# Spectral ffn image by image: groups of 16 bins and bursts of four steps in a ring of half PSUM banks

## The chip, the cores and the metric

The kernel runs on one core of a Trainium2 chip. The metric is the device time of the execution in microseconds; lower is better. Three runs of the kernel before gave 2106.07, 2108.23 and 2112.26 us (median 2108.23). All data are fp32.

## What is computed

x has shape (2, 128, 64, 64). Three blocks follow one another; the change touches only the last one.

```python
x = x + conv_ref(_gn(x), ...)                 # neighbourhood attention and an mlp
t = _to_tokens(x)                             # (2, 4096, 128)
t = t + attn_ref(_ln_t(t))                    # full attention over 4096 tokens
t = t + ffn_ref(_ln_t(t), ...)                # spectral filter ("stu")

# ffn_ref, for one branch:
Vf = rfft(phi, n=8192, axis=0)                # 16 filters in time
Uf_p = rfft(u, n=8192); Uf_m = rfft(u * sgn, n=8192)
U_plus  = irfft(Vf * Uf_p)[:sl]
U_minus = irfft(Vf * Uf_m)[:sl] * sgn
out = einsum('btkd,k,kde->bte', U_plus, s, Mpp) + einsum('btkd,k,kde->bte', U_minus, s, Mpm)
out = out + three short lags u[t-i] @ Mu[i]
```

Four such branches (over the whole, half, quarter and eighth of the sequence) are weighted by a hard softmax choice.

## The kernel before

Layer 0 and the attention of layer 1 come first, up to about 1296 us of the trace. While attention runs on image 1, the spectra of the tokens are stored to a DRAM tile `us` (line 1045 and 1050) and those of the filters to a DRAM tile `gs`; the matrices `mpl` and `mmi` (16 matrices of 128 by 128 each, sum and difference of the two sets) and the inverse transform `inv` are made in SBUF.

The last stage is the ffn in the frequency domain. There are `K2` = 80 indices q, each with four bins (j = 0 to 3). Both images are worked on together. One group takes `KG` = 2 indices (kl), so there are 40 groups.

- **Loads** (`blocks`, line 1335, and `inputs`, line 1405). For each kl SyncE issues four DMAs for the filter block `ct` (40 or 32 KB) and one for `ut`, the spectra of both images (256 KB, pieces of 2 KB). Four kl are loaded ahead, in five buffers.
- **Burst** (line 1430). A Toeplitz product of filter block and spectrum, for one kl and one image: for par 0 and 1, four products with 32 contraction rows each (row slices of the array, j = 0 to 3), 256 columns, into four PSUM banks. par 0 and par 1 fill the two interleaved parts of the same four banks. Then four copies of 128 by 512 (line 1438) bring the banks to `y`, j even on VectorE, j odd on ScalarE. A group has four bursts (two kl times two images); they compute the `y` of the following group.
- **Projection** (line 1450). 32 products with 128 contraction rows, 256 columns, accumulate `acc` over l (mpl, mmi) and the 16 filters. A burst for the next group stands ahead of every eight projections.
- **Mixed bins** (lines 1458 to 1477). ScalarE copies `acc` to `af`; POOL (VectorE in the last group) forms eight sums and differences and puts them into `ob` (the first 64 indices) or `ob_last` (the other 16).
- **Back transform** (`back_into`, lines 1484 to 1500). When 64 indices are done, each of the 16 places (image, par, f) gets four transposes into one bank, one copy to `t`, then four products with `inv` and two adds into the residual `xa`. These steps are slipped in behind projections k = 5 and 13, in groups 32 to 39.
- **Tail** (lines 1548 to 1592). Behind the last group: 16 transposes of `ob_last`, then four turns (half h, image b) of residual products, 32 products with `inv`, eight copies or adds into `o` and a store of 1 MB.

TensorE's order in the loop is the order of the program text (`manual_schedule`); the other engines' instructions are ordered by the framework. PSUM has eight banks of 512 fp32 columns: here `ps_c` is a ring of six banks for bursts, transposes and back products, and `ps_p` two buffers for `acc`. An fp32 product shows in the trace as two TensorE instructions.

Of the kernel before, what the change touches and what calls it, by code (L numbers as in the profile page):

```python
# [96 lines left out]
KG = 8 // FB  # L97
GB = 4 * KG
# [5 lines left out]
def kernel(  # L104
# [1290 lines left out]
    with ExitStack() as cv:  # L1395
        cp = cv.enter_context(tc.tile_pool(name="conv", bufs=5))
        ps_c = cv.enter_context(tc.tile_pool(name="ps_c", bufs=6, space=PSUM))
        ps_p = cv.enter_context(tc.tile_pool(name="ps_p", bufs=2, space=PSUM))
        def lag_bank():
            return ps_c.tile([P, 512], F32, tag="pc", name="py")  # L1400

        def inputs(q):

            ut = cp.tile([P, NB, 2, P], F32, tag="ut", name="ut")
            nc.sync.dma_start(
                out=ut.rearrange("p b s d -> p (b s d)"),
                in_=us[2 * q : 2 * q + 2].rearrange("g n i r f b s d -> (g n i r f) (b s d)"),
            )
            return ut

        TK = FB * KF
        GROUPS = K2 // KG
        NX = 8 // FB
        UNITS = [(kl, images) for kl in range(KG) for images in (((0,), (1,)) if FB == 4 else ((0, 1),))]
        taken = []

        def burst(y, i):

            kl, images = UNITS[i]
            if images[0] == 0:  # L1420
                taken[:] = ahead.pop(0)
            ct, ut = taken
            pcs = [ps_c.tile([P, 2, 2 * NX, TK], F32, tag="pc", name="pc") for _ in range(4)]
            for i_, b in enumerate(images):
                for par in range(2):
                    cv_ = ct[:, :, 0 : 2 * (FB + 1 + par) * KF].rearrange("p o (l c) -> p o l c", l=2)[:, :, :, 0:TK]
                    at = slice(2 * i_ + par, 2 * i_ + par + (NX - 1 if par else NX + 1) + 1, NX - 1 if par else NX + 1)
                    for j in range(4):
                        rows_ = slice(32 * j, 32 * j + 32)
                        nc.tensor.matmul(  # L1430
                            pcs[j][:, :, at, :], lhsT=ut[rows_, b, par, :], rhs=cv_[rows_], start=True, stop=True
                        )
            for j in range(4):
                if FB == 4:
                    to = y[:, :, :, 4 * kl + j, images[0] * 2 * FB : (images[0] + 1) * 2 * FB]
                else:
                    to = y[:, :, :, 4 * kl + j, :]
                (nc.scalar.copy if j % 2 else nc.vector.tensor_copy)(  # L1438
                    to, pcs[j].rearrange("p o (l x) (t k) -> p (o l) k (x t)", l=2, k=KF)
                )  # L1440
            if to_load and images[-1] == 1:
                q_ = to_load.pop(0)
                ahead.append((blocks(q_), inputs(q_)))

        def new_y():
            return cp.tile([P, 4, KF, GB, 4 * FB], F32, tag="y", name="y", bufs=2)

        def project(g, y, acc, l, k):

            nc.tensor.matmul(  # L1450
                acc, lhsT=(mmi if l else mpl)[:, k, :],
                rhs=y[:, l::2, k], start=(l == 0 and k == 0), stop=(l == 1 and k == KF - 1),
            )

        def mixed_bins(g, acc):
# [3 lines left out]
            eng = nc.gpsimd if g + 1 < GROUPS else nc.vector  # L1459
            av = af.rearrange("p (m s x) -> p s m x", s=2, x=4 * FB)  # L1460
            sd = cp.tile([P, 2, 128], F32, tag="sd", name="sd", bufs=2)
            for s, op in enumerate((ALU.add, ALU.subtract)):
                to = sd[:, s, :].rearrange("p (o x k) -> p o k x", o=2, x=4 * FB)
                a_, b_ = (av[:, i].rearrange("p (o k) x -> p o k x", o=2) for i in range(2))
                eng.tensor_tensor(to, a_, b_, op)  # L1465
            sv, dv = (sd[:, s].rearrange("p (o x k e) -> p e o x k", o=2, k=KG, e=2) for s in range(2))
            c, k0 = divmod(g * KG, BC)
            if c < K2 // BC:
                to = [ob[:, c, a].rearrange("p x k o -> p o x k")[:, :, :, k0 : k0 + KG] for a in range(4)]
            else:  # L1470
                to = [ob_last[:, :, a].rearrange("p x k o -> p o x k")[:, :, :, k0 : k0 + KG] for a in range(4)]
            eng.tensor_tensor(to[0], sv[:, 0], sv[:, 1], ALU.add)
            eng.tensor_tensor(to[1], sv[:, 0], sv[:, 1], ALU.subtract)
            eng.tensor_tensor(to[2][:, 0], dv[:, 0, 0], dv[:, 1, 1], ALU.subtract)
            eng.tensor_tensor(to[2][:, 1], dv[:, 0, 1], dv[:, 1, 0], ALU.add)
            eng.tensor_tensor(to[3][:, 0], dv[:, 0, 0], dv[:, 1, 1], ALU.add)
            eng.tensor_tensor(to[3][:, 1], dv[:, 0, 1], dv[:, 1, 0], ALU.subtract)

        def back_into(chunk, b, par, f):

            pt = ps_c.tile([P, 4, P], F32, tag="pc", name="pt")
            for a in range(4):
                src = ob[:, chunk, a, (b * 2 + par) * FB + FB - 1 - f]
                nc.tensor.transpose(pt[:, a, :], src.rearrange("p k o -> p (k o)"), ident)
            t = cp.tile([P, 4, P], F32, tag="t", name="t", bufs=4)
            nc.scalar.copy(t, pt)
            yield True
            na = 512 // CQ
            for a0 in range(0, 4, na):
                py = ps_c.tile([P, na, CQ], F32, tag="pc", name="py")  # L1490
                for a in range(na):
                    nc.tensor.matmul(
                        py[:, a, :], lhsT=t[:, a0 + a, :], rhs=inv[:, 4 * chunk + a0 + a, :], start=True, stop=True
                    )
                xv = xa[b][:, par * TH : (par + 1) * TH].rearrange(
                    "p (h x e f c l) -> p x f e l h c", x=NFP, e=2, f=2, c=64, l=2
                )[:, f // 2, f % 2]
                for a in range(0, na, 2):
                    xs = xv[:, (a0 + a) // 2]
                    nc.vector.tensor_tensor(xs, py[:, a : a + 2, :].rearrange("p l (h c) -> p l h c", c=64), xs, ALU.add)  # L1500
                yield None if a0 + na == 4 else True

        places = [(b, par, f) for b in range(NB) for par in range(2) for f in range(FB)]
        to_load = list(range(K2))
        ahead = [(ct, inputs(to_load.pop(0))) for ct in first_blocks]
        rest = []
        with tc.manual_schedule(engines={mybir.EngineType.PE}):
            y = new_y()
            for i in range(4):
                if i % 2 == 0:  # L1510
                    next(lags, None)
                burst(y, i)
# [6 lines left out]
            ob = obp.tile([P, K2 // BC, 4, 4 * FB, BC, 2], F32, name="ob")  # L1519
            ob_last = obp.tile([P, 4 * FB, 4, LAST, 2], F32, name="ob_last")  # L1520
            for g in range(GROUPS):
                following = new_y() if g + 1 < GROUPS else None
                acc = ps_p.tile([P, 256], F32, tag="acc", name="acc")
                for l in range(2):
                    for k in range(KF):
                        if following is not None and k % 8 == 0:
                            burst(following, 2 * l + k // 8)
                        project(g, y, acc, l, k)
# [3 lines left out]
                mixed_bins(g, acc)  # L1532
                y = following
                if (g + 1) * KG % BC == 0:
                    rest += [back_into(g * KG // BC, *p) for p in places]
# [5 lines left out]

        turned_ = {}
        for b in range(NB):
            for par in range(2):
                pt = ps_c.tile([P, FB, P], F32, tag="pc", name="pt")
                for f in range(FB):
                    src = ob_last[:, (b * 2 + par) * FB + FB - 1 - f]
                    nc.tensor.transpose(pt[:, f, :], src.rearrange("p a k o -> p (a k o)"), ident)
                turned_[b, par] = cp.tile([P, 4, P], F32, tag="t", name="t", bufs=4)
                nc.scalar.copy(turned_[b, par][:, 0:FB], pt)  # L1550
        HQ = CQ // 2
        for h in range(2):
            for b in range(NB):
                o = cp.tile([P, HQ, 2, 2, FB, 2], F32, tag="o", name="o", bufs=2)
                pys = [ps_c.tile([P, 2, FB, HQ], F32, tag="pc", name="py") for _ in range(4)]
                xv = [
                    xa[b][:, par * TH + h * (TH // 2) : par * TH + (h + 1) * (TH // 2)].rearrange(
                        "p (h x e f c l) -> p e l x f h c", x=NFP, e=2, f=2, c=64, l=2
                    )
                    for par in range(2)  # L1560
                ]

                def residual(par, a):
                    v = xv[par][:, a // 2, a % 2]
                    return v[:, :, :, 0] if FB == 4 else v[:, 0]

                def alike(v):
                    return v.rearrange("p (x f) c -> p x f c", f=2) if FB == 4 else v.rearrange("p f (h c) -> p f h c", c=64)

                for a in (0, 2):  # L1570
                    for par in range(2):
                        nc.tensor.matmul(
# [115 lines left out]
```

## Time and profile before

| what | value |
|---|---|
| median of three runs | 2108.23 us |
| the profiled execution's own time | 2109.33 us |
| its span in the trace | 2107.4 us |
| TensorE granted clock, mean | 0.992 |
| span before the first burst of the ffn | 1295.85 us |
| first to last projection | 1307.3 to 2078.9 us |
| behind the last projection | 28.5 us |

Times are microseconds from the span's start. PE is TensorE's products, PEld its weight loads, DVE is VectorE, ACT ScalarE, POOL GpSimd, SPq the DMA-issuing queue of SyncE. A timeline row has start, duration, engine, line, operation, names as output<-inputs, shapes, a count, and in brackets the engine's idle time before it and what ended it. A row of waits has the waiting engine, its tile and line, what it waited for, the total, the number of times and the longest. A row of stretches has, behind its length, each engine's busy time with its instructions in the order PE, PEld, DVE, ACT, POOL, then the granted clock, the DMA engines' busy share and GB/s.

### The profile page before, as it was taken

To read this page: it belongs to the slowest core of one execution; us is meant where nothing else is said; L and a number is where in the kernel's file an instruction comes from. 1 tells how busy PE (TensorE), PEld (TensorE's weight loads), DVE (VectorE), ACT (ScalarE), POOL (GpSimd) and SP (SyncE) were. 2 spreads that over 40 slices of the span, in tenths; PEclk is the share of its full clock that TensorE was granted. 3 is DMA by queue.
4 is the path that set the end of the run, shared out by engine and by line. 5 is a ranking of instruction groups with operands and counts; after the bars stand their busy time and mean duration, and the time that the engine had idled before them with its cause. 6 is when DMAs were issued, how large, how long until landed. Compare 5 with 4: busy or idle time off the path is not lost.

```text
span 2107.4 us, 36450 instructions
## 1 busy us (share of the span) xinstructions
PE 2042.4 (97%) x13704; PEld 1336.8 (63%) x13704; DVE 962.1 (46%) x3368; ACT 727.1 (35%) x1942; POOL 397.0 (19%) x703
## 2 busy tenths in 40 slices
PE   6899998999999999999999999999999999999998
PEld 4677775554555554554455555777777777777877
DVE  5799986444543455346534455222222222222332
ACT  3788985222322233122222322222222222222222
POOL 3366976214000000000000000110111111110100
PEclk8999999999999999999999999999999999999999
DMA  4222223012000011004200013111111111111102
GB/s 148 62 61 61 62 60 54 6 42 83 22 4 25 26 41 57 4 27 124 70 8 18 26 51 99 40 48 41 46 43 45 48 40 48 41 46 40 40 9 81
DMA packets 181839, 99.96 MB, mean 47 GB/s; under 512 B 70927, under 2 KB 169375, under 8 KB 181152
## 3 DMA queue, kind: packets, MB, share of 16 engines
q1 hardware_dynamic: 180738, 94.13, 16.1%
q8 instruction: 109, 1.79, 0.3%
q0 software_dynamic: 576, 2.10, 0.3%
q10 hardware_dynamic: 350, 1.41, 0.3%
q14 instruction: 66, 0.54, 0.1%
HBM read 62.98 MB, written 34.63 MB: 46 GB/s over the span
## 4 chain that ended last, share of the span: by engine, by line
PE 82%; DVE 6%; DMA 4%; POOL 4%; ACT 1%; issue 1%; SPq 1%; ACTq 0%; DVEq 0%; POOLq 0%
PE acc L1450 28%; PE own L958 10%; PE bank L920 9%; PE pc L1430 8%; PE other L985 8%; PE bank L944 4%; PE bank L345 2%; PE bank L203 1%; PE bank L555 1%; PE bank L1060 1%; DMA st<-in_m_plus_dram 1%; DMA st<-in_m_minus_dram 1%; PE bank L1103 1%; ACT p L542 1%; PE bank L519 1%
## 5 line engine op out<-in xcount | busy, mean ns | idle before, releaser
L1438 DVE COPY y<-pc 128x512 f32<-128x512 f32 x320 | 206.2, 686 | 514.9 <-PE pc L1430 395.4
L928 ACT ACTIVATE e<-bank 128x512 f32<-128x512 f32 (+3 forms) x288 | 161.7, 561 | 518.9 <-PE bank L920 396.0
L1438 ACT COPY y<-pc 128x512 f32<-128x512 f32 x320 | 171.8, 589 | 445.5 <-PE pc L1430 432.2
L1450 PE MATMUL acc<-y,mpl 128*128 128x256 f32 x1280 | 299.9, 385 | 0.0
L1450 PE MATMUL acc<-y,mmi 128*128 128x256 f32 x1280 | 299.9, 385 | 0.0
L920 PE MATMUL bank<-cm 128*128 128x512 f32 (+3 forms) x576 | 277.7, 565 | 1.4 <-DVE y L666 1.4
L1450 PEld LDWEIGHTS acc<-y,mpl 128*128 128x128 f32 x1280 | 235.5, 190 | 54.1 <-issue 25.9
L1450 PEld LDWEIGHTS acc<-y,mmi 128*128 128x128 f32 x1280 | 235.5, 190 | 54.1 <-issue 25.9
L958 PE MATMUL own<-et,tok 128*128 128x512 f32 x448 | 230.3, 600 | 7.6 <-DVE part L947 7.3
L985 PE MATMUL other<-e,tok 128*128 128x512 f32 x448 | 229.3, 594 | 4.6 <-DVE xa L997 4.6
L947 DVE CUSTOM_DVE_ANT_0 et<-bank,one 128x512 f32<-128x512 f32 x224 | 146.1, 687 | 128.8 <-PE bank L944 128.6
L1430 PE MATMUL pc<-ct,ut 32*128 32x256 f32 x2560 | 186.2, 403 | 3.4 <-DMA ut<-us 3.2
L1465 POOL TENSOR_TENSOR sd<-af 128x128 f32<-128x128 f32 x78 | 34.3, 464 | 700.1 <-ACT af L1458 650.7
L958 PEld LDWEIGHTS own<-et,tok 128*128 128x128 f32 x448 | 82.7, 190 | 120.9 <-issue 60.9
L1430 PEld LDWEIGHTS pc<-ct,ut 32*128 32x128 f32 x2560 | 118.2, 185 | 61.4 <-issue 56.1
L175 POOL TENSOR_TENSOR ln_rs<-ln_rs,mhalf 128x4 f32<-128x4 f32 x24 | 24.2, 1010 | 702.8 <-DVE ln_rs L174 702.8
L985 PEld LDWEIGHTS other<-e,tok 128*128 128x128 f32 x448 | 81.7, 190 | 95.2 <-issue 87.3
L944 PEld LDWEIGHTS bank<-ident,e 128*128 128x128 f32 x896 | 103.0, 141 | 46.1 <-issue 39.4
L920 PEld LDWEIGHTS bank<-cm 128*128 128x128 f32 x576 | 94.4, 191 | 54.2 <-issue 39.2
L542 ACT ACTIVATE p<-p,mn 128x196 f32<-128x196 f32 x256 | 114.4, 449 | 14.3 <-DVE mn L532 13.8
L944 PE MATMUL bank<-ident,e 128*128 128x128 f32 x896 | 117.0, 274 | 0.0
L1041 DVE TENSOR_TENSOR ub<-bank,uo 128x256 f32<-128x256 f32 (+1 forms) x192 | 59.5, 372 | 71.1 <-ACT uo L1038 70.2
(246 smaller groups left out, 2419.8 us busy)
## 6 DMA issues: line engine op xcount, KB each, us to landing
ut<-us SPq DMA_DIRECT2D x80, 256.0 KB
us<-ub SPq DMA_DIRECT2D x128, 128.0 KB
vw<-vd SPq DMA_DIRECT2D x256, 49.0 KB
ct<-gs SPq DMA_DIRECT2D x160, 40.0 KB
ct<-gs SPq DMA_DIRECT2D x160, 32.0 KB
vd<-v SPq DMA_DIRECT2D x128, 32.0 KB
st<-in_m_plus_dram SPq DMA_DIRECT2D x16, 256.0 KB
us<-ub SPq DMA_DIRECT2D x128, 32.0 KB
```

Of the source, the lines that this page charges most:

```text
L345: nc.tensor.matmul(pl, lhsT=wg[:, lo : lo + P], rhs=zT, start=True, stop=True)
L542: nc.scalar.activation(p, p, AF.Exp, bias=t[name + "mn"][:, h : h + 1], scale=-1.0, accum_out=t["den"][:, u, h : h + 1],)
L920: nc.tensor.matmul(ps[:, lo:], lhsT=cm[b][:, n * P : (n + 1) * P], rhs=cm[b][:, CHUNKS[c] * 512 + lo : (CHUNKS[c] + 1) * 512], start=True, ...
L928: nc.scalar.activation(e[:, lo:], ps[:, lo:], AF.Exp, bias=0.0, scale=ASCALE, accum_out=part[:, n, c : c + 1])
L944: nc.tensor.transpose(pt[:, k * P : (k + 1) * P], es[k][:, m * P : (m + 1) * P], ident)
L947: nc.vector.tensor_tensor_reduce(et, pt, one, 1.0, 0.0, ALU.mult, ALU.add, part[:, n, a : a + 1])
L958: nc.tensor.matmul(own, lhsT=tok[b][:, n, :], rhs=e, start=first, stop=last)
L985: nc.tensor.matmul(other, lhsT=tok[b][:, 4 * CHUNKS[a] + j, :], rhs=es[j], start=(j == 0), stop=(j == 3))
L1041: nc.vector.tensor_tensor(ub[:, sgn, 0:n], pu[s][:, 0:n], half[:, 0:n], op)
L1430: nc.tensor.matmul(pcs[j][:, :, at, :], lhsT=ut[rows_, b, par, :], rhs=cv_[rows_], start=True, stop=True)
L1438: (nc.scalar.copy if j % 2 else nc.vector.tensor_copy)(to, pcs[j].rearrange("p o (l x) (t k) -> p (o l) k (x t)", l=2, k=KF))
L1450: nc.tensor.matmul(acc, lhsT=(mmi if l else mpl)[:, k, :], rhs=y[:, l::2, k], start=(l == 0 and k == 0), stop=(l == 1 and k == KF - 1),)
```

## The change

- The ffn is done image by image: 20 groups of `KG` = 4 indices (16 bins) for image 0, then 20 for image 1. `ut` holds one image (pieces of 1 KB), so `ct` and `ut` are loaded once for each image and index: 160 times five DMAs instead of 80 times five.
- A burst covers two kl: four steps (kl, par) of four products each, two bursts a group instead of four. The products are the same in number and size (32 of 256 columns a group).
- PSUM is one tile of eight banks with two halves of 256 columns each. Seven banks are a ring of 14 places: place n is bank n mod 7, half (n div 7) mod 2. Each product of a burst has a place of its own, with a copy of 128 by 256: 32 copies a group instead of 16 of twice the size. The eighth bank holds `acc`, in alternating halves.
- `y`, `ob` and `ob_last` are laid out anew; a transpose now reads its source with a stride of four elements.
- The back transform uses two places with two transposes (or products) each where it used a bank. It follows at groups 16 to 19 of each image.
- Image 0's last 16 indices and its output (`finished`) are done in the first groups of image 1, with all four quarters added on VectorE and without residual products. The tail does image 1 alone, with whole banks as before.

```diff
-        ps_c = cv.enter_context(tc.tile_pool(name="ps_c", bufs=6, space=PSUM))
-        ps_p = cv.enter_context(tc.tile_pool(name="ps_p", bufs=2, space=PSUM))
+        ps = cv.enter_context(tc.tile_pool(name="ps_c", bufs=1, space=PSUM)).tile([P, 8, 2, 256], F32, name="ps_c")
+        RING = 7
+        at_slot = [0]
+        def slot():
+            n = at_slot[0]
+            at_slot[0] += 1
+            return ps[:, n % RING, n // RING % 2, :]
...
-        def inputs(q):
-            ut = cp.tile([P, NB, 2, P], F32, tag="ut", name="ut")
+        def inputs(b, q):
+            ut = cp.tile([P, 2, P], F32, tag="ut", name="ut")
...
-        def burst(y, i):
-            kl, images = UNITS[i]
...
+        def burst(y, kls):
+            for kl in kls:
+                ct, ut = ahead.pop(0)
                 for par in range(2):
...
+                    pcs = [slot() for _ in range(4)]
                     for j in range(4):
                         rows_ = slice(32 * j, 32 * j + 32)
                         nc.tensor.matmul(
-                            pcs[j][:, :, at, :], lhsT=ut[rows_, b, par, :], rhs=cv_[rows_], start=True, stop=True
+                            pcs[j].rearrange("p (l o c) -> p o l c", l=2, o=2), lhsT=ut[rows_, par, :], rhs=cv_[rows_],
+                            start=True, stop=True,
                         )
...
+                    for j in range(4):
+                        n = 4 * kl + j
+                        at = slice(2 * n + 1, 2 * n + 33, 31) if par else slice(2 * n, 2 * n + 34, 33)
+                        (nc.scalar.copy if j % 2 else nc.vector.tensor_copy)(
+                            y[:, :, at, :], pcs[j].rearrange("p (l x k) -> p k l x", l=2, k=KF)
+                        )
+                if to_load:
+                    b_, q_ = to_load.pop(0)
+                    ahead.append((blocks(q_), inputs(b_, q_)))
...
+        def finished(b):
+            ts = []
+            for par in range(2):
+                ts.append(turned(b, par))
+                yield True
+            for h in range(2):
+                o = cp.tile([P, HQ, 2, 2, FB, 2], F32, tag="o", name="o", bufs=2)
+                for par in range(2):
+                    pys = [slot().rearrange("p (f q) -> p f q", f=FB) for _ in range(4)]
+                    for f in range(FB):
+                        for a in range(4):
+                            last_products(pys[a], ts[par], h, f, a, True)
+                    for a in range(4):
+                        nc.vector.tensor_tensor(
+                            alike(place_of(o, par, a)), alike(pys[a]), residual(b, par, h, a), ALU.add
+                        )
+                    if par:
+                        send(b, h, o)
+                    yield None if h and par else True
...
+            groups = [(b, g) for b in range(NB) for g in range(GROUPS)]
+            for i, (b, g) in enumerate(groups):
+                final = i + 1 == len(groups)
+                following = None if final else new_y()
+                acc = ps[:, RING, i % 2, :]
                 for l in range(2):
                     for k in range(KF):
-                        if following is not None and k % 8 == 0:
-                            burst(following, 2 * l + k // 8)
-                        project(g, y, acc, l, k)
+                        if following is not None and k == 0:
+                            burst(following, (2 * l, 2 * l + 1))
+                        project(y, acc, l, k)
...
+                if g + 1 == GROUPS and not final:
+                    rest.append(finished(b))
```

## The prediction

> **What bounds the kernel now.** I read the page's busy shares first, then three stretches of the run, then the timeline inside one period of the long stretch.
>
> ```profile
> PE 2042.4 (97%) x13704; PEld 1336.8 (63%) x13704; DVE 962.1 (46%) x3368; ACT 727.1 (35%) x1942; POOL 397.0 (19%) x703
> ...
> 1307.31:1907.60 600.29, 600.29 (x4067) 467.32 (x4065) 163.37 (x254) 147.70 (x285) 70.56 (x248) 1.00 0.17 45
> 1907.60:2078.90 171.30, 171.20 (x1172) 138.69 (x1168) 49.47 (x90) 43.51 (x82) 18.20 (x64) 1.00 0.09 25
> 2078.90:2107.40 28.50, 19.45 (x304) 16.68 (x304) 9.05 (x24) 10.59 (x21) 0.00 (x0) 0.84 0.37 149
> ```
>
> The change lies wholly in the ffn stage, which is those last 800 us: TensorE is busy all through it at full granted clock, VectorE and ScalarE for a quarter, the DMA engines for 0.17. So the stage lasts as long as TensorE's instruction stream, gaps included. The timeline shows one period, a burst of 16 instructions (8 products in two passes) and 16 projection instructions:
>
> ```profile
> 1500.03 1.15 PE L1430 MATMUL pc<-ct,ut 32*128 32x256 f32 x16
> 1501.10 3.72 PE L1450 MATMUL acc<-y,mpl 128*128 128x256 f32 x16
> 1501.19 1.29 DVE L1438 COPY y<-pc 128x512 f32<-128x512 f32 x2 [3.38 <-PE pc L1430]
> 1501.23 1.07 ACT L1438 COPY y<-pc 128x512 f32<-128x512 f32 x2 [3.61 <-PE pc L1430]
> ...
> 1504.75 1.15 PE L1430 MATMUL pc<-ct,ut 32*128 32x256 f32 x16
> ```
>
> The period is 4.727 us (127 of them between 1307.4 and 1907.7). Without a burst ahead, 16 projection instructions take 3.46 us in the chain of waits, 0.216 each. In a burst four instructions run side by side (start times a few ns apart), so it is four rounds of 0.216. That sums to 3.46 + 0.86 = 4.32; the missing 0.41 us is the change of shape: read instruction by instruction, the two starts behind each change come 0.31 to 0.32 apart instead of 0.216, four times a period. The view of waits has the same thing on the weight loads:
>
> ```profile
> PEld acc L1450 <- issue: 51.7, 156, 0.3
> PEld pc L1430 <- issue: 51.4, 155, 0.3
> ```
>
> Copies are over 1.4 us after the burst; the next burst is 3.6 us off, so TensorE never waits for one here.
>
> **The change, part by part.** Everything is summed against the profiled execution's own 2109.3 us (span 2107.4), which lies 1.1 above the median of 2108.2.
>
> *Fewer changes of shape.* 39 groups go from four bursts to two, 78 times 0.41 = 32 us less, if a burst of twice the length runs without a gap: 0.32 + 6 x 0.216 + 0.32 = 1.94 us, call it 1.97 with issue times.
>
> *The ring.* This is where I think it goes wrong. A burst now fills 16 half banks in a row, 256 columns each; place n lies in bank n mod 7, so n and n+7 share a bank. Does n+7's product wait for n's copy, though they touch different halves? The tail of this trace answers. There a bank holds par 0 in one half and par 1 in the other; ScalarE's first copy reads par 0 alone, done in the middle of the 2 us of products, and ScalarE is idle:
>
> ```profile
> 2086.07 2.01 PE L1580 MATMUL py<-inv,t 32*128 32x64 f32 x64
> ...
> 2088.10 2.00 ACT L1591 COPY o<-py 128x256 f32<-128x256 f32 x4 [3.47 <-PE py L1580]
> 2088.14 1.98 DVE L1589 TENSOR_TENSOR o<-py,xa 128x256 f32<-128x256 f32 x4 [7.55 <-PE py L1580]
> ```
>
> It starts 0.02 us after the last product ends, and only the last four products raise a semaphore at all. The same holds at L1012: of four transposes into four quarters of a bank only the last signals, and the first reader of a quarter waits for it. So this program's waits go by bank, and 14 halves are a ring of seven. The Trainium skill, "PSUM — Partial Sum Buffer", section "PSUM bank collisions raise a hardware error", says that engines must be kept apart by bank (and quadrant), not by address; it speaks against the ring for the same reason, and by it the sum is the one below. The skill's "Perfetto Trace Analysis", section "Matmul Optimizations", asks for all eight banks to be in use; by that rule alone seven banks instead of six should help, and the sum would be the 32 us saved; the rows here show six banks without a wait, so I don't follow it.
>
> What a burst costs then is set by VectorE's copies. A 256-column copy is priced by these rows:
>
> ```profile
> L777 DVE COPY add<-bank x1: 425/425/425, 49.2 to 49.2; 128x256 f32<-128x256 f32 x1
> ...
> L1500 DVE TENSOR_TENSOR xa<-py,xa x32: 414/420/426, 1921.3 to 2078.3; 128x256 f32<-128x256 f32 x32
> ...
> L1038 ACT COPY uo<-bank x96: 266/373/381, 471.0 to 1282.7; 128x256 f32<-128x256 f32 x64, 128x128 f32<-128x128 f32 x32
> ```
>
> Back to back, the second L1500 starts 0.342 behind the first, and L1038 0.269. From the burst's first product: the first step's second passes start at 0.32, last 0.374, and the copy starts 0.04 later, at 0.735. VectorE's copies (places 0, 2, 4, 6, 8) then start every 0.342; place 8's starts at 0.735 + 4 x 0.342 = 2.10, ends at 2.53, and 0.05 later (the lag seen between a copy's end and the weight load that it frees) place 15 starts, at 2.58. Two passes of 0.32 bring the first projection at 3.23 us. On the way places 7, 9, 11, 13 and 14 wait too (1.22, 1.56, 1.90, 2.24, 2.40), so VectorE is fed in time. The method can be tried on this trace: ahead of the stage three bursts run in a row through six banks,
>
> ```profile
> 1304.73 0.90 PEld L1430 LDWEIGHTS pc<-ct,ut 32*128 32x128 f32 x16 [0.27 <-DVE y L1438]
> ...
> 1306.25 0.73 PEld L1430 LDWEIGHTS pc<-ct,ut 32*128 32x128 f32 x12 [0.62 <-DVE y L1438]
> ```
>
> where the same reckoning with 0.686 and 0.608 per copy gives 4.48 us from first product to first projection, and 1302.83 to 1307.31 is 4.48. Those gaps of 0.3 to 0.9 us left the products' duration at 374 ns, so the granted clock should not fall.
>
> Half a group is then 3.23 + 32 projection instructions (32 x 0.216 + 0.20 at the changes = 7.11) = 10.34 us, a group 20.68 against 4 x 4.727 = 18.91: 1.77 more, times 39 = **+69 us**. Bounds: a copy every 0.30 us gives a burst of 3.0 and +51; one that takes 0.42 with no overlap gives 3.5 and +93. Inside that lies the wait for the second kl's five loads: up to three semaphore instructions of 51 ns, 0.1 apart, sit in mid-burst behind a blocked load, 0 to 0.15 us a burst, 0 to +12.
>
> *Twice the loads.* Each kl loads five DMAs per image instead of per pair: 800 for 400. SyncE's queue needs 3.0 us for five (0.51 to 0.60 each, once 1.67), 4.3 at worst, and gets 5.2 per kl; four kl, 20 us, are loaded ahead; the DMA share goes from 0.17 to about 0.3. Cost nothing, hidden by that lead; without the lead a kl would cost what the queue takes beyond its 5.2 us, which at 4.3 is still nothing.
>
> *Start.* The first products now wait for ut of image 0 alone. The last store of us (image 1's) is issued at 1288.5, the ut loads at 1293.1 behind its landing, the burst begins at 1295.85. TensorE is free at 1292.7, so 0 to 3.2 us to gain, depending on whether the wait tells the images apart in one DRAM tile; I take 1.5. The first four old bursts and a lag step, 11.5 us at clock 0.84, become two long ones and the lag step: about 1.5 less. Sum -3.
>
> *Tail and mid-stage.* The tail loses half of 16 transposes (3.2 us) and two of four turns of 4.05 us (residual products, products): -9.7; the last copy, store and landing (7 us) stay. Image 0's part comes into the next image's first groups: eight transposes at 0.6 for four, four product steps of 1.0 us (half of 2.0) with a change of shape of 0.41 each: +6.9. Its adds (0.46 apart at L1589, four a step) and POOL's bins (2.4 us behind af, 4.7 us before the first transpose) are over before anything needs them. The stores on SyncE wait for those adds with the loads queued behind, some 3 us against the 20 of lead. Net -2.8.
>
> *Both acc in one bank.* By the same waits a group's first projection stands behind af's copy (373 ns) of the group before; a burst covers it in all but the last group: +0.7.
>
> *Strided sources and small copies.* The transposes now read every fourth element. No row has that; L1572 reads every second at 2.0 us for eight, no slower than projections. 80 transposes at 0 to +0.1: 0 to +9, taken as 0, the nearest row's. Split copies of t and POOL's new strides are off the path.
>
> Sum: 2109.3 + 69 - 3 - 2.8 + 0.7 = 2173; less the 1.1, **2172 us**.
>
> **Rivals.** *The halves are free of each other* (faster): place 14 then waits for place 0's copy, done at 1.16, needed at 1.4. Burst 1.97, group 18.16, 39 x -0.75 = -29, with the rest -34: 2074. For it: nothing but the layout, which puts neighbours in different banks; against it the tail rows. It turns where a burst takes 2.4 us, that is, where the last place is free at 1.76 instead of 2.58. *The whole of PSUM is one tile and waits as one* (slower yet): each step waits for the copies before it, 1.55 us a step, and projections for the burst's last copy: half a group 13.3, +300 us, 2400. The rows of a bank can't exclude it, as no tile of before has several banks. *Short of copies, but less so* (starts overlap the waits, bursts of 2.45 to 2.85 us): 39 times 0.2 to 1.0, with the rest 2110 to 2142.
>
> **How the numbers follow.** The forecast gets 0.80, free halves 0.11, one big tile 0.04, the mild case 0.05. The forecast's own range, from +51 and from +93 with the strides, is 2150 to 2210; 2120 to 2210 leaves out the two outer rivals and little else. Chances at the 0.3% that this kernel's runs can tell: faster 0.12, same 0.02, slower 0.86.
>
> **What would show it.** Weight loads at the burst's line idle behind the copies of y, some 1.2 us a burst, and TensorE's share of the stage falls by a tenth; burst to burst 10.3 us; copies of y at 425 and 373 ns; the tail from last bins to end near 19 us instead of 28. Wrong if no burst waits for a copy and the group is near 18.2 us, or if SyncE's queue is what the weight loads wait for.

## The result and the profile after

The changed kernel takes 2182.16 us (median of four runs, 2180.47 to 2187.02) against 2109.35 for the kernel before: 1.0349 times the time, interval 1.0326 to 1.0373. It is slower by 3.5 per cent; 2172 was predicted. The profiled execution of the changed kernel is the slowest of its four (2187.02 us), so its span of 2185.1 us is 77.7 more than before where the medians differ by 72.8. Its page and three stretches of it, from the first burst on:

```profile
PE 2117.5 (97%) x13688; PEld 1421.7 (65%) x13688; DVE 986.6 (45%) x3696; ACT 765.1 (35%) x2274; POOL 395.7 (18%) x703
...
1297.30:1313.50 16.20, 14.86 (x102) 9.84 (x102) 9.42 (x28) 7.72 (x23) 0.00 (x0) 0.79 0.27 72
1313.53:2168.70 855.17, 848.37 (x5354) 693.57 (x5354) 238.81 (x665) 231.41 (x692) 88.31 (x312) 1.00 0.20 53
2168.70:2185.10 16.40, 9.49 (x153) 7.61 (x151) 5.03 (x16) 5.45 (x13) 0.00 (x0) 0.83 0.32 129
```

The busy share of TensorE is 97% as before, and the granted clock in the stretch of projections is still 1.00: neither shows that anything is wrong. What grew is the stretch of projections, by 83.7 us (first to last projection 771.1 before, 854.8 now). The timeline of one burst of four steps shows where:

```profile
1508.68 0.74 PEld L1434 LDWEIGHTS ps_c<-ct,ut 32*128 32x128 f32 x14 [0.33 <-issue]
1508.68 3.41 PE L1434 MATMUL ps_c<-ct,ut 32*128 32x256 f32 x32
1509.41 2.92 DVE L1441 COPY y<-ps_c 128x256 f32<-128x256 f32 x8 [7.52 <-PE ps_c L1434]
1509.45 0.92 ACT L1441 COPY y<-ps_c 128x256 f32<-128x256 f32 x3 [7.40 <-PE ps_c L1434]
1509.89 1.80 PEld L1434 LDWEIGHTS ps_c<-ct,ut 32*128 32x128 f32 x18 [0.47 <-DVE y L1441]
...
1512.02 0.48 PE L1453 MATMUL ps_c<-y,mmi 128*128 128x256 f32 x1
```

Fourteen weight loads (seven products, two passes each) go out at once. The fifteenth, of the eighth product, waits for VectorE's first copy of `y`: it starts at 1509.89, 1.21 us into the burst. From there the burst goes at the pace of the copies, and the first projection comes 3.34 us after the first product instead of 1.94. TensorE's row is unbroken all the same: each product is drawn some 0.4 us long from its start, so the wait leaves only 0.07 us uncovered (1509.82 to 1509.89). The waits before weight loads, from 1330 to 2050 us, have a new first row; the first line here is of the kernel before, the others are of the changed one:

```profile
PEld pc L1430 <- issue: 49.4, 149, 0.3
...
PEld ps_c L1434 <- DVE y L1441: 31.8, 66, 0.5
PEld ps_c L1453 <- issue: 22.2, 67, 0.3
PEld ps_c L1434 <- issue: 21.6, 65, 0.3
```

The idle time at changes of shape (issue) is about half of what it was, as intended: some 67 pairs of changes instead of 149 in that stretch. The wait for the copies took its place and more. 31.8 us understates it: only whole gaps of the weight loads count there, not the thinner stream behind the first gap.

Read off the start times of single instructions, as medians over the stage:

| kernel | first product to first projection, us | half a group (16 products of a burst, 16 of projection), us | median us | ratio to before |
|---|---|---|---|---|
| before | 1.076 (twice) | 9.454 | 2109.35 | |
| changed | 3.339 | 10.443 | 2182.16 | 1.0349 |
| e1, one half of each bank | 3.341 | 10.445 | 2183.53 | 1.0359 |
| e2, seven copies a burst | 1.939 | 9.043 | 2074.95 | 0.9848 |
| e3, two steps a burst | 1.836 (twice) | 10.974 | 2222.70 | 1.0549 |
| e7, before with joined bursts | 3.000 | 10.104 | 2156.92 | 1.0237 |
| e4, pairs in a bank | 3.033 | 10.138 | 2155.70 | 1.0230 |
| e5, image by image, old bursts | 1.076 (twice) | 9.454 | 2104.20 | 0.9980 |
| e6, e5 with two loose ends tied | 1.076 (twice) | 9.454 | 2100.99 | 0.9966 |
| e8, eight banks | 1.939 | 9.043 | 2070.81 | 0.9823 |

Ratios are to the kernel before on the same chip (2107.1 to 2107.4 us there). 78 half groups hold a burst, so 78 x (10.443 - 9.454) = 77.1 us of the 83.7 by which the stretch grew are the bursts.

### The profile page after: what moved, and what is told of

Same layout as the page of the kernel before. It is cut to its first block, busy times and chain, and to the rows that moved or that the text cites. A ratio compares the mean times of both kernels' runs of the same rounds, so it can differ in the third digit from the quotient of the medians.

```text
span 2185.1 us, 37755 instructions
## 1 busy us (share of the span) xinstructions
PE 2117.5 (97%) x13688; PEld 1421.7 (65%) x13688; DVE 986.6 (45%) x3696; ACT 765.1 (35%) x2274; POOL 395.7 (18%) x703
## 4 chain that ended last, share of the span: by engine, by line
PE 82%; DVE 7%; DMA 4%; POOL 3%; ACT 1%; issue 1%; SPq 1%; DVEq 0%; POOLq 0%; ACTq 0%
PE ps_c L1453 26%; PE ps_c L1434 11%; PE own L956 10%; PE bank L918 9%; PE other L983 8%; PE bank L942 4%; PE bank L343 2%; DVE y L1441 1%; PE bank L201 1%; PE bank L553 1%; PE bank L1058 1%; DMA st<-in_m_minus_dram 1%; DMA st<-in_m_plus_dram 1%; PE bank L1101 1%; ACT p L540 1%
## 5 line engine op out<-in xcount | busy, mean ns | idle before, releaser
L1441 DVE COPY y<-ps_c 128x256 f32<-128x256 f32 x640 | 226.7, 416 | 492.6 <-PE ps_c L1434 485.6
L1441 ACT COPY y<-ps_c 128x256 f32<-128x256 f32 x640 | 213.0, 375 | 330.2 <-PE ps_c L1434 308.8
L1453 PE MATMUL ps_c<-y,mpl 128*128 128x256 f32 x1280 | 290.5, 382 | 0.5 <-ACT af L1461 0.5
L1453 PE MATMUL ps_c<-y,mmi 128*128 128x256 f32 x1280 | 290.0, 382 | 0.0
L1434 PE MATMUL ps_c<-ct,ut 32*128 32x256 f32 x2560 | 267.8, 414 | 10.2 <-DMA ut<-us 2.6
L1453 PEld LDWEIGHTS ps_c<-y,mpl 128*128 128x128 f32 x1280 | 238.5, 190 | 44.0 <-issue 12.9
L1453 PEld LDWEIGHTS ps_c<-y,mmi 128*128 128x128 f32 x1280 | 238.7, 190 | 43.2 <-issue 12.9
L1434 PEld LDWEIGHTS ps_c<-ct,ut 32*128 32x128 f32 x2560 | 195.0, 184 | 78.4 <-DVE y L1441 37.3
L540 ACT ACTIVATE p<-p,mn 128x196 f32<-128x196 f32 x256 | 114.4, 449 | 14.3 <-DVE mn L530 13.8
L1461 ACT COPY af<-ps_c 128x256 f32<-128x256 f32 x40 | 14.9, 372 | 259.1 <-PE ps_c L1453 259.1
```

The source lines that it names most:

```text
L540: nc.scalar.activation(p, p, AF.Exp, bias=t[name + "mn"][:, h : h + 1], scale=-1.0, accum_out=t["den"][:, u, h : h + 1],)
L1434: nc.tensor.matmul(pcs[j].rearrange("p (l o c) -> p o l c", l=2, o=2), lhsT=ut[rows_, par, :], rhs=cv_[rows_], start=True, stop=True,)
L1441: (nc.scalar.copy if j % 2 else nc.vector.tensor_copy)(y[:, :, at, :], pcs[j].rearrange("p (l x k) -> p k l x", l=2, k=KF))
L1453: nc.tensor.matmul(acc, lhsT=(mmi if l else mpl)[:, k, :], rhs=y[:, k, 32 * l : 32 * l + 32].rearrange("p n x -> p (n x)"), start=(l == 0 ...
```

## The experiments

The theory: a place of the ring can be written again only when the last copy out of its bank is done, whichever half that copy reads. So 14 half banks are seven places, and a burst of 16 goes at the pace of the copies. The rivals: the halves are free of each other and the stalls come from elsewhere (the second kl's loads and their semaphores in mid-burst, the doubled loads), or the length of a burst itself costs.

**e1: do the second halves do anything?**

```diff
-            return ps[:, n % RING, n // RING % 2, :]
+            return ps[:, n % RING, 0, :]
```

> The changed kernel, but every place of the ring is the first half of its bank (seven places of 256 columns, the second halves never used). By-bank theory: the second halves buy nothing, so nothing moves: 2182 us within 4, half a group 10.44 us. Rival (14 halves work as 14 places and the stalls come from elsewhere): half the places are gone, each burst waits some 1.3 us more, near 2280 us.

2183.53 us (1.0359, interval 1.0341 to 1.0376), as the changed kernel's 1.0349. The same burst with half of the ring's space unused:

```profile
1506.20 0.74 PEld L1434 LDWEIGHTS ps_c<-ct,ut 32*128 32x128 f32 x14 [0.33 <-issue]
1506.20 3.41 PE L1434 MATMUL ps_c<-ct,ut 32*128 32x256 f32 x32
1506.93 2.92 DVE L1441 COPY y<-ps_c 128x256 f32<-128x256 f32 x8 [7.52 <-PE ps_c L1434]
...
1507.41 1.79 PEld L1434 LDWEIGHTS ps_c<-ct,ut 32*128 32x128 f32 x18 [0.47 <-DVE y L1441]
```

Row by row it is the burst above. The second halves buy nothing; the ring has seven places. What TensorE waits for is a semaphore of the copy, so this is shown of the program as it is built; no run leaves these waits out, and whether a product and a copy could use the two halves of a bank at the same time stays open.

**e2: is it the copies?** TensorE's products stay, nine of the sixteen copies of a burst are left out, and no product stands behind a copy of its own burst. The parts of `y` that get no copy hold zeros, in two buffers that are cleared once ahead of the stage.

```diff
-                    pcs = [slot() for _ in range(4)]
+                    step = 2 * (kl % 2) + par
+                    pcs = [ps[:, 4 + j if step == 3 and j < 3 else j, step % 2, :] for j in range(4)]
...
                     for j in range(4):
+                        if step < 2 or (step, j) == (2, 3):
+                            continue
...
```

> The changed kernel with the copies of a burst's first nine products but the last three of step three left out (16 products, seven copies: three of the third step, all four of the fourth; the rest of y keeps zeros, so part of the result is left out), placed so that no product of a burst stands behind a copy of the same burst. TensorE does the same products. By-bank theory: a burst takes 1.97 to 2.1 us, half a group 9.1 to 9.2, the whole 2076 to 2086 us, some 30 below the kernel before: the saving of the fewer changes of shape, bare. Rival (the stalls come from the second kl's loads, their semaphores in mid-burst or the doubled DMA): bursts stay near 3.3 us and the time above 2150.

2074.95 us (0.9848, interval 0.9828 to 0.9868).

```profile
1507.88 1.61 PEld L1435 LDWEIGHTS ps_c<-ct,ut 32*128 32x128 f32 x32 [0.33 <-issue]
1507.89 2.01 PE L1435 MATMUL ps_c<-ct,ut 32*128 32x256 f32 x32
...
1509.82 2.24 PEld L1461 LDWEIGHTS ps_c<-y,mpl 128*128 128x128 f32 x11 [0.33 <-issue]
```

All 32 weight loads are one block, and the burst takes 1.94 us. The loads, their semaphores and the number of products are those of the changed kernel, so the whole 1.40 us a burst hung on the copies. And 78 x (9.043 - 9.454) = -32.1 us is what fewer changes of shape are worth where nothing else is in the way.

**e3: fewer steps a burst, more bursts.** One kl a burst, four bursts a group, the ring as it is.

```diff
-                        if following is not None and k == 0:
-                            burst(following, (2 * l, 2 * l + 1))
+                        if following is not None and k % 8 == 0:
+                            burst(following, (2 * l + k // 8,))
```

> The changed kernel with one kl (two steps, eight places) a burst and four bursts a group, the ring as it is. By-bank theory: place 7 waits for place 0's copy, so the burst takes 1.9 us instead of 1.08, a group 22.1 us instead of 20.9: 2225 to 2240 us. Rival (only the number of changes of shape counts): four changes as before the change, 18.9 us a group, near 2105 us.

2222.70 us (1.0549, interval 1.0528 to 1.0570).

```profile
1503.39 1.91 PE L1434 MATMUL ps_c<-ct,ut 32*128 32x256 f32 x16
...
1504.61 0.29 PEld L1434 LDWEIGHTS ps_c<-ct,ut 32*128 32x128 f32 x2 [0.48 <-DVE y L1441]
```

A single product of eight waits for a copy, and that alone makes the burst 1.84 us instead of 1.08. The time is 2.3 us under the expected range, since the burst takes 1.84 us where 1.9 was expected, 156 times.

**e7: the kernel before, its bursts joined.** Nothing of the change but the joining.

```diff
-                        if following is not None and k % 8 == 0:
-                            burst(following, 2 * l + k // 8)
+                        if following is not None and k == 0:
+                            burst(following, 2 * l)
+                            burst(following, 2 * l + 1)
```

> The kernel before with the two bursts of each half group run one behind the other (two bursts of 8 products through the six banks, then 16 products of projection); nothing else changed. By-bank theory: the second burst finds two free banks and waits for 512-column copies; 2.99 us from first product to first projection, half a group 10.1 instead of 9.45: +50, 2160 us. Rival (fewer changes of shape save 0.41 us each, 78 times): 2077 us.

2156.92 us (1.0237, interval 1.0217 to 1.0258); 3.00 us a burst.

```profile
1508.63 1.16 PEld L1430 LDWEIGHTS pc<-ct,ut 32*128 32x128 f32 x20 [0.33 <-issue]
...
1510.59 0.73 PEld L1430 LDWEIGHTS pc<-ct,ut 32*128 32x128 f32 x12 [0.80 <-DVE y L1438]
```

Six whole banks and 512-column copies fail for the same reason: what a joined burst needs beyond its free banks waits for a copy. For a loss of this kind, neither going image by image nor the half banks nor the doubled loads are needed.

**e4: the two products of a row slice (par 0 and 1) share one bank, with one copy of 512 columns.** A burst needs eight banks, and seven are there.

```diff
-                for par in range(2):
+                pcs = [next_bank() for _ in range(4)]
+                for par in range(2):
...
-                    pcs = [slot() for _ in range(4)]
+                    at = slice(1, 3) if par else slice(0, 4, 3)
...
-                            pcs[j].rearrange("p (l o c) -> p o l c", l=2, o=2), lhsT=ut[rows_, par, :], rhs=cv_[rows_],
+                            pcs[j].rearrange("p (r o c) -> p o r c", r=4, o=2)[:, :, at, :], lhsT=ut[rows_, par, :],
...
+                        y.rearrange("p k (h n) x -> p k h (n x)", h=2)[:, :, :, 16 * n : 16 * n + 16],
+                        pcs[j].rearrange("p (h m k) -> p k h m", h=2, k=KF),
```

> The changed kernel, bursts of four steps as they are, but par 0 and par 1 of a product share a bank (two halves, same row slice) and one copy of 512 columns takes both, in a ring of seven banks: eight banks a burst, so only the eighth product pair waits, for the first bank's 512-column copy. By-bank theory: that copy ends at 1.85 us, the first projection follows at 2.98; half a group 10.1 us, 2150 to 2160 us. Rival (14 halves work as 14 places, or the stalls come from the loads): no different from the changed kernel, 2182 us.

2155.70 us (1.0230, interval 1.0211 to 1.0248).

```profile
1507.27 1.57 PE L1440 MATMUL ps_c<-ct,ut 32*128 32x256 f32 x22
...
1508.50 1.29 DVE L1446 COPY y<-ps_c 128x512 f32<-128x512 f32 x2 [7.29 <-PE ps_c L1440]
...
1509.24 0.72 PEld L1440 LDWEIGHTS ps_c<-ct,ut 32*128 32x128 f32 x10 [0.81 <-DVE y L1446]
```

22 passes go at once; the ones left wait until the first 512-column copy is out (1508.50 + 0.69 + 0.05 = 1509.24). One bank too few costs 1.09 us a burst.

**e5: the rest of the change without its bursts.** e4's pairs, with one kl a burst and four bursts a group as in e3's diff. Image by image, the doubled loads and the output of image 0 in mid-stage stay.

> The changed kernel with the old bursts: one kl a burst, four a group, par 0 and 1 in the halves of one bank, one 512-column copy each, seven banks. Image by image, twice the loads, and the output of image 0 in mid-stage stay. By-bank theory: no burst waits, the group is 18.9 us as before; the tail gives 12 us, the mid-stage part takes 7, the start 0 to 4 more: 2102 to 2109 us. Rival (going image by image with twice the loads is what costs): above 2130 us.

2104.20 us (0.9980, interval 0.9971 to 0.9989): a hair faster than before. In the waits no copy stands before a weight load any more, and half a group is 9.454 us:

```profile
PEld ps_c L1459 <- issue: 49.1, 148, 0.3
PEld ps_c L1440 <- issue: 48.4, 146, 0.3
```

So the loss of 3.5 per cent lies in the bursts, and the doubled loads cost nothing that can be seen.

**e6: e5 with two loose ends at the start of the stage tied.** One DRAM tile of spectra for each image; and the lag step takes a place of its own. In the changed kernel `lag_bank` counts up first and so takes the bank in which the next burst begins.

```diff
-    us = dram.tile([Q, 2, 2, SG, FB, NB, 2, P], F32, name="us")
+    us = [dram.tile([Q, 2, 2, SG, FB, 2, P], F32, name=f"us{b}") for b in range(NB)]
...
-            at_slot[0] += 1
-            return whole_bank(at_slot[0] % RING)
+            return next_bank()
```

> As the one with the old bursts, and the spectra in one DRAM tile for each image, so that the first loads of image 0 don't stand behind the last stores of image 1; and the lag step takes a bank of its own in the ring, not the one that the next burst begins with. Expected: the first burst begins 3 to 4 us earlier, 2097 to 2105 us; if the loads are late for another reason, the same as the one with the old bursts.

2100.99 us (0.9966, interval 0.9953 to 0.9978); the interval overlaps that of e5. From first burst to first projection the profiled run takes 11.4 us instead of e5's 14.3. 1.2 of that is the lag bank: in e5 TensorE stands idle for 1.22 us behind the lag step's adds into `xa`, and in e6 it doesn't. The other 1.8 is the granted clock of the two profiled runs: the six lag products take 4.62 us at 0.61 in e5 and 2.84 us at 1.00 in e6. The first half of the expectation did not come true as meant: the loads of `ut`, issued at 1290.10, still wait for the landing of image 1's last store (issued at 1285.79, landed at 1289.96) though they read another DRAM tile, and for the last lag product, which ends at 1290.00. Why they do was not tried; it could be the SBUF space that `ut` takes over.

**e8: the eighth bank.** Two kl a burst again and pairs in a bank as in e4, with e6's DRAM tiles, and all eight banks. `acc` is summed over 16 projections instead of 32, and moves on: it takes the bank that ScalarE empties first, and the next burst comes to it last.

```diff
+            first = at_slot[0] if acc_at[0] is None else acc_at[0] + 1
+            for i_, kl in enumerate(kls):
                 ct, ut = ahead.pop(0)
-                pcs = [next_bank() for _ in range(4)]
+                pcs = [whole_bank((first + 4 * i_ + j) % 8) for j in range(4)]
...
+        def new_acc():
+            n = ((at_slot[0] if acc_at[0] is None else acc_at[0] + 1) + 1) % 8
+            acc_at[0] = n
+            at_slot[0] = n + 1
+            return ps[:, n, 0, :]
...
-                start=(l == 0 and k == 0), stop=(l == 1 and k == KF - 1),
+                start=(k == 0), stop=(k == KF - 1),
...
+            nc.vector.tensor_tensor(af, acc, af, ALU.add)
...
+                    if l == 0:
+                        af = half_sum(acc)
```

> Bursts of four steps again, but with no bank lacking: as the one with a DRAM tile for each image, par 0 and 1 in the halves of a bank, one 512-column copy each, two kl a burst in all eight banks. To free the eighth, acc is summed over 16 projections instead of 32: the first half's sum goes to af on ScalarE, the second half's is added to it on VectorE, and acc moves on round the banks (it takes the second bank of each burst, copied first by ScalarE; the next burst comes to that bank last). By-bank theory: no burst waits, 1.94 us a burst and 9.04 us half a group as where nine copies were left out; 78 times 0.41 less than with the old bursts: 2068 to 2078 us, faster than the kernel before by 1.5 per cent. Rival (a long burst costs by its length, banks or not): half a group stays near 10 us, 2140 us or more.

2070.81 us (0.9823, interval 0.9804 to 0.9841): 1.8 per cent faster than the kernel before.

```profile
1501.01 1.61 PEld L1441 LDWEIGHTS ps_c<-ct,ut 32*128 32x128 f32 x32 [0.33 <-issue]
1501.01 2.01 PE L1441 MATMUL ps_c<-ct,ut 32*128 32x256 f32 x32
1501.29 0.42 DVE L1479 TENSOR_TENSOR af<-ps_c,af 128x256 f32<-128x256 f32 x1 [5.67 <-PE ps_c L1467]
...
1502.95 6.77 PEld L1467 LDWEIGHTS ps_c<-y,mpl 128*128 128x128 f32 x32 [0.33 <-ACT y L1447]
```

All 32 loads in one block, and the same 1.939 and 9.043 us as with the copies left out in e2. The burst has the same products as the one that lost 3.5 per cent. Against e4, which joins the same bursts in the same pairs, the stage has the eighth bank, the split sum and the DRAM tiles of its own, and the tiles change nothing in it (9.454 us in e5 and in e6): half a group takes 9.043 us instead of 10.138. The added 0.42 us on VectorE lies beside the burst. The first projection now names ScalarE's copy as what it waited for, but its 0.33 us is that of any change of shape: the bank is free just in time.

## Why the prediction was right, point by point

- **The ring, +69 us.** Right in mechanism, 8 us short in size. The eighth place started 1.21 us into the burst (reckoned 1.22), the tenth 1.54 (1.56), the fourteenth 2.20 (2.24), the fifteenth 2.37 (2.40). The ninth, which by the same reckoning follows at 1.22, came at 1.50. Behind the blocked load of the eighth stand three semaphore instructions of the second kl's loads, at 1509.89, 1510.00 and 1510.10, and the ninth product's load comes right behind them, at 1510.18, although ScalarE had emptied its bank at 1509.83. Its copy, the fifth on VectorE, starts 0.17 late, and the sixteenth product at 2.71 instead of 2.58. That is the term that the prediction put at 0 to 0.15 us a burst and took as nothing. Copies that follow one another every 0.332 us instead of 0.342 took some of it back, which was luck; 0.11 a burst is left, or 8 us. This is read from the trace; no run takes the three instructions away and leaves the copies.
- **Fewer changes of shape, 32 us.** e2 and e8 show 32.1 (78 times 0.411).
- **Waits go by bank.** Read from the tail of the trace before, and shown by e1. The Trainium skill's rule ("PSUM — Partial Sum Buffer", section "PSUM bank collisions raise a hardware error"), to guard PSUM by bank and quadrant and not by address, fits these runs. The other rule weighed there is to use all eight banks ("Perfetto Trace Analysis", section "Matmul Optimizations"). Every kernel here uses all eight, so that rule alone does not tell them apart. What counts is how many a burst has: a seventh bank in the ring gains nothing while it is still too short (half a group 10.138 us in e4, 10.104 in e7), and the eighth, which ends the waits, is worth 78 x 1.095 = 85 us (e8 against e4).
- **Price of a copy.** 0.425 and 0.373 us reckoned; medians 0.415 on VectorE and 0.372 on ScalarE.
- **Twice the loads, nothing.** Right by e5; the DMA share over the whole stretch of projections went from 0.15 to 0.20, where the prediction had 0.17 going to 0.3.
- **Start, -3 us.** Wrong: +6.2 in the profiled runs. 1.4 of it is a first burst that came later; in runs that share the code ahead of it that time lies between 1293.3 (e4) and 1297.3, so nothing is read from it. 4.8 is the way from first burst to first projection (16.2 against 11.5). The second long burst begins in the bank that the lag step holds, which is 1.2 us of idle time. The lag step itself runs at a lower granted clock here, 4.94 us for its six products where the kernel before took 2.8. The first line is of the kernel before:

```profile
1300.05:1302.83 2.78, 2.78 (x9) 1.06 (x7) 0.98 (x2) 0.81 (x2) 0.00 (x0) 1.00 0.11 27
...
1301.33:1306.27 4.94, 4.94 (x7) 1.85 (x6) 0.26 (x1) 0.37 (x1) 0.00 (x0) 0.57 0.31 79
...
1306.31 1.13 DVE L1117 SCALAR_TENSOR_TENSOR xa<-ps_c,seg,xa 128x128 f32<-128x128 f32 x4 [4.71 <-PE ps_c L1101]
1307.48 0.74 PEld L1434 LDWEIGHTS ps_c<-ct,ut 32*128 32x128 f32 x14 [2.24 <-DVE xa L1117]
```

  These 2.1 us can't be put down to the change: with the same lag step the clock was 1.00 in the profiled runs of e4 and e6 and 0.61 in that of e5. The last 1.5 us, with the stalls of the two long bursts in them, are not taken apart here. The earlier load of image 0 did not come either, and by e6 it wouldn't have with separate tiles.
- **Tail, -9.7 us.** It was -12.2. The residual products of the first half moved ahead of the last bins and are hidden by them, 2 us that had not been counted:

```profile
2168.56 1.98 PE L1607 MATMUL ps_c<-xa,ident 128*128 128x256 f32 x8
...
2169.32 0.49 DVE L1465 TENSOR_TENSOR sd<-af 128x128 f32<-128x128 f32 x2 [0.92 <-ACT af L1461]
```

- **Image 0's output in mid-stage and the last acc, +7.6 us.** 83.7 - 77.1 = 6.6. Strided transposes taken as 0: four take 0.63 us instead of 0.60.

Sum of the profiled runs: +6.2 + 83.7 - 12.2 = 77.7, against +64 reckoned (69 - 3 - 2.8 + 0.7); the 8 us of the ring and the 9 of the start are the difference, less 2.5 of the tail and 1 of the mid-stage.

Two of the signs that the prediction named did not come. The weight loads idle behind the copies for 0.47 us a burst and not for 1.2, since the later waits of a burst overlap weight loads that go on; and TensorE's share of the stretch fell from 100% to 99% (848.37 of 855.17 us), not by a tenth. The time from burst to burst did come near, 10.44 us where 10.3 was named.

## What to carry to other kernels

Count a ring in PSUM by banks, not by places: in this program a second half was no second buffer while a copy out of the first still ran. Before joining short bursts to save changes of shape, count the banks that the joined burst writes before its first copy can end; one bank too few cost 1.09 us a burst here, more than twice the 0.41 that joining saves. When one bank is lacking, look at what holds the others: splitting a long sum in two freed the bank for the price of one 0.42 us add a group, and turned e4's 2.3 per cent slower into 1.8 per cent faster.

## What was not expected of the hardware

- A TensorE that waits again and again can look fully busy: 97% in both kernels, and a burst that lost 1.4 us shows one gap of 0.47 us in its weight loads (0.55 at most). Start-to-start times show it.
- The three semaphore instructions of a kl cost nothing where the load ahead of them does not wait: in e8 they stand at 1501.03 to 1501.25 and the burst's 32 weight loads are one block. Behind the blocked weight load of the changed kernel they held the next product's load back by 0.3 us.
- The repeated stalls did not lower the granted clock: it is 1.00 from first to last projection of the changed kernel, with an idle 0.47 us of the weight loads every 10.44 us, and a product of its bursts still takes 374 ns in the median.
